# Value products for two quads at a time in a cross-attention kernel: a change read from its trace

## The chip, the cores and the metric

The kernel runs on one core of one Trainium2 chip. The metric is the device time of one execution in microseconds (us), taken as the median over runs. In the profile the engines are PE (TensorE matmul), PEld (TensorE weight load), DVE (VectorE), ACT (ScalarE), POOL (GpSimd) and SP (SyncE, which issues nearly all DMAs here).

## What is computed

The reference is a layer norm, a query projection, cross-attention with 32 heads over a context that serves as keys and as values, an output projection and a residual. Shapes: 8 batches, 256 query rows, 256 context rows, 1024 columns, everything in float32.

```python
x = (hidden - mean) * rsqrt(var + 1e-5) * gamma + beta
Q = split_heads(x @ Wq.T)                 # 32 heads of 32
K = V = split_heads(ctx)
scores = einsum('bhsd,bhtd->bhst', Q, K) * 32 ** -0.5
probs = softmax(where(mask, scores, -inf), axis=-1)
attn = einsum('bhst,bhtd->bhsd', probs, V)   # heads put side by side again
out = hidden + attn @ Wout.T
```

## The kernel before

**Quads and slots.** The work is cut into 64 quads: quad n is batch n // 8 and four heads (128 columns) of it. The main loop (L670) has 64 slots; the order of every instruction on every engine is the order in which the program writes it (L113), so what is queued where can be read from the loop body. Slot n does, on PE in this order: the scores of quad n+1 (`scores`, L354, tile `sc`), the value products of quad n-2 (`values`, L484, tile `pv`), a first group of output-product steps (`product_steps`, L543, tile `po`), one query projection for a quad some six slots ahead (`make_q`, L310, tile `pq`) and a second group of output-product steps. `STEPS` (L520) says how many steps fall in the two groups, by i = n % 8: for most batches (0,4), (0,3), (1,3), (1,2), (2,2), (2,1), (3,1), (0,3). The output product of a batch comes a batch later than its attention, as seven half-size products in Strassen's manner; its operand sums S1, S3, S2 (slot i = 1) and S4 (slot i = 2) are made by POOL (`sum_at`, L532). Float32 matmuls stand as two instructions each in the trace, so the 32 matmuls of `values` are 64.

**Softmax.** `softmax_parts` (L373) for quad n+1 runs in slot n, on four engines. For each of its four heads j, `exps(j)` has DVE take the masked scores out of PSUM with their row minimum (L396) and ACT exponentiate them with the row sums (L400). Then DVE makes the reciprocals (L407), POOL scales (L409), DVE transposes 32x32 blocks into `pT` (`blocks`, L415), and ACT puts half of `pT` aside in `pc` (`aside`, L421) so that two pairs of DMAs (L472, L476) can exchange partition groups. The loads due in the slot (`between`) are issued between the two pairs. DVE's order is exps(0), exps(1), exps(2), reciprocal 0, exps(3), reciprocal 1, blocks(0), and so on. ACT's order is exps(0), then the copies of finished value products out of PSUM (`copy_at`, L499, into `at`), then exps(1) to exps(3), aside, `copy_q`, aside. After the softmax, DVE makes the layer-norm statistics or blocks of a later batch, and POOL the sums.

**Buffers.** `sc` takes four PSUM banks, each for one head of a quad. `pv` has two banks (L104): a quad fills both, one for each half r of the partitions[...]. `pq` and `po` have a bank each. `pT` has three buffers, `pc` three. The mask of all batches is loaded by one DMA of 256 KB at the start (L186), as the seventh on the SP queue, ahead of the second x, of seven of the eight blocks of Wq and of the first values; `mask_bias` (L349) turns one batch of it into an additive bias.

**Evacuations.** A `po` bank is read by DVE (`keep` L561, `store` L569) or ACT (L559) before the next product may begin in it. In slots i = 2 and 3 DVE does this after exps(3) (`hooks[0]`), in slots i = 4, 5, 6 after blocks(0) (`hooks[1]`); the second group of steps of the slot waits for it. In the last batch's slots (56 to 63) the evacuation stands ahead of the softmax on DVE (L714). In slots above 58 there is no query projection left, and each slot adds one chunk of the last batch's own output projection (`project`, L572), for quads that are already copied to `at`. Values of the quads 62 and 63 and the rest of the projections follow the loop (L769 on).

The early slots (0 to 7) carry more: two query projections in some of them, POOL's folds of gamma into Wq (L342) and its sums of Wout blocks (L177).

Of the kernel before, what the change touches and what calls it, by code (L numbers as in the profile page):

```python
# [47 lines left out]
U8 = mybir.dt.uint8  # L48
# [11 lines left out]
def xattn_kernel(  # L60
# [34 lines left out]
    qp = ctx.enter_context(tc.tile_pool(name="qp", bufs=8))  # L95
    atp = ctx.enter_context(tc.tile_pool(name="atp", bufs=2))
    ep = ctx.enter_context(tc.tile_pool(name="ep", bufs=4))
    ptp = ctx.enter_context(tc.tile_pool(name="ptp", bufs=3))
    asp = ctx.enter_context(tc.tile_pool(name="asp", bufs=3))
    up = ctx.enter_context(tc.tile_pool(name="up", bufs=1))  # L100
    sm = ctx.enter_context(tc.tile_pool(name="sm", bufs=12))
    PS = bass.MemoryType.PSUM
    ps_s = ctx.enter_context(tc.tile_pool(name="ps_s", bufs=4, space=PS))
    ps_v = ctx.enter_context(tc.tile_pool(name="ps_v", bufs=2, space=PS))  # L104
# [33 lines left out]
    def load_v(n):  # L138
# [4 lines left out]
            vs[n], kv[b, g // 2, :, 2 * T :].rearrange("p (i v) -> p i v", i=NI)  # L143
        )

    def load_res(b, s, h):
        rs[b, s, h] = rp.tile([P, 512], F32, tag="r", name=f"r_{b}_{s}_{h}")
        nc.sync.dma_start(rs[b, s, h], x[b, ts(s, P), ts(h, 512)])
# [5 lines left out]
    mk = const.tile([P, B, T], U8, tag="mk", name="mk")  # L154
    NK = NC // 2
    wo = const.tile([P, 7, NK, 512], F32, tag="wo", name="wo")
    B11, B21, B22, T1, T2, T3, T4 = range(7)
# [191 lines left out]
    def mask_bias(b):  # L349

        mbs[b] = sm.tile([P, T], F32, tag="mb", name=f"mb_{b}", bufs=2)
        nc.vector.tensor_scalar(mbs[b], mk[:, b, :], 1.0, -MASKED, ALU.subtract, ALU.mult)

    def scores(n, part=range(NS)):  # L354
        if 0 in part:
# [17 lines left out]
    def softmax_parts(n, new_q=(), between=(), hooks={}, fill=()):  # L373
# [49 lines left out]
        if n == 0:  # L423
            for j in range(NH - 1):
                exps(j, (0,))
            yield
            exps(NH - 1, (0,))
            fill_in()
            yield
            for j in range(NH):  # L430
                exps(j, (1,))
            normalize(0)
            fill_in()
        else:
# [46 lines left out]
            tail()  # L481
        yield

    def values(n):  # L484
        pvs[n] = [
            ps_v.tile([P, 2, NS, K], F32, tag="pv", name=f"pv_{n}_{r}") for r in range(2)
        ]
        pT = pTs.pop(n)
        for i in range(NI):
            for j in range(NH):  # L490
                for r in range(2):
                    nc.tensor.matmul(  # L492
                        pvs[n][r][j * HD : (j + 1) * HD],
                        vs[n - n % 2][ts(r, 2 * K), i, ds(n % 2 * P + j * HD, HD)],
                        pT[ts(r, 2 * K), :, i, j, :, :],
                        start=(i == 0), stop=(i == NI - 1),
                    )

    def copy_at(n):  # L499
        b, c = divmod(n, NQ)  # L500
        if c == 0:
            ats[b] = atp.tile([P, NC, NS, NA, K], F32, tag="at", name=f"at_{b}")
        for r, pv in enumerate(pvs.pop(n)):
            nc.scalar.copy(  # L504
                ats[b][:, c, :, ts(r, 2), :], pv.rearrange("p a s k -> p s a k")
            )

# [88 lines left out]
        made += k  # L596


    loads, stats, norms, trans, moves, biases = ({n: [] for n in range(N)} for _ in range(6))
    for b in range(1, B):  # L600
        first = next(n for n in range(N) if b * NQ in new_qs[n])
        if b == 1:
            when = dict(moves=())
        elif b == 2:
            when = dict(
                loads=(0, 1), stats=(2, 3), norms=(3, 3), trans=(4, 4),
                moves=tuple(4 + i // 4 for i in range(16)),
            )
        else:
            when = dict(  # L610
                loads=(first - 12, first - 11), stats=(first - 10, first - 9),
                norms=(first - 8, first - 7), trans=(first - 7, first - 6),
                moves=tuple(first - 5 + i // 4 for i in range(16)),
            )
# [12 lines left out]


    sums = {n: [] for n in range(N)}
# [40 lines left out]
    for n in range(N):  # L670
# [156 lines left out]
```

## Time and profile before

| what | value |
|---|---|
| median of 3 runs | 595.76 us (595.75 to 595.84) |
| the profiled execution, its own time | 596.43 us |
| span of its profile | 594.6 us |
| PE busy | 582.0 us, 98% |
| PE weight loads busy | 389.3 us, 65% |
| DVE busy | 458.3 us, 77% |
| ACT busy | 407.0 us, 68% |
| POOL busy | 347.5 us, 58% |
| DMA queue of SP | 99.91 MB, 57.4% of 16 engines |

The span runs from the first instruction to the last; the execution's own time has 1.83 us more around it. A row of the profile gives an engine, a source line, the tiles written and read, a count, and the busy time. A row of the timeline gives the start, the length, and in brackets how long the engine sat idle before and what released it. Matmuls are pipelined, so neighbouring rows of PE overlap by some tenths of a microsecond; a group's cost is read from one start to the next. The granted clock is full in all slices of the profile.

### The profile page before, as it was taken

What the parts mean: (1) busy time and instruction counts of PE and PEld (TensorE: products, weight loads), DVE (VectorE), ACT (ScalarE), POOL (GpSimd) and SP (SyncE); (2) the same over time, 40 slices, a digit from 0 to 9 for tenths busy, and PEclk for the clock granted to TensorE, in tenths of its full rate; (3) what the DMA queues carried; (4) which work ended last, traced back from release to release, by engine and by line L of the source; (5) the groups of instructions that cost most, each with busy time, mean ns of one, the idle gap of its engine ahead of it and who ended that gap; (6) DMA issues with size and microseconds to landing.
All of it is one profiled execution on the core that took longest, in us unless ns stands there. A gap on an engine that the chain in (4) does not pass through costs nothing.

```text
span 594.6 us, 18914 instructions
## 1 busy us (share of the span) xinstructions
PE 582.0 (98%) x6680; PEld 389.3 (65%) x6680; DVE 458.3 (77%) x1675; ACT 407.0 (68%) x1380; POOL 347.5 (58%) x630
## 2 busy tenths in 40 slices
PE   9999999999999999999999999999999999999997
PEld 8787776666666676666676667666666667654443
DVE  5878888697887878788787887878787677779801
ACT  4788786776777776686676876677677677667700
POOL 1568896987557644755447653484556564385600
PEclk9999999999999999999999999999999999999999
DMA  8566798545863667544674457654556355466541
GB/s 309 222 165 210 227 255 234 156 114 172 228 185 90 175 177 209 167 113 139 195 225 128 130 157 191 193 155 136 158 145 194 99 162 142 125 181 174 165 126 71
DMA packets 42063, 101.13 MB, mean 170 GB/s; under 512 B 8560, under 2 KB 8560, under 8 KB 41968
## 3 DMA queue, kind: packets, MB, share of 16 engines
q1 hardware_dynamic: 41680, 99.91, 57.4%
q8 instruction: 53, 0.87, 0.7%
q14 instruction: 42, 0.34, 0.2%
q10 hardware_dynamic: 288, 0.01, 0.0%
HBM read 51.65 MB, written 8.39 MB: 101 GB/s over the span
## 4 chain that ended last, share of the span: by engine, by line
PE 76%; POOL 12%; DVE 5%; issue 2%; DMA 2%; ACT 2%; SPq 1%; POOLq 0%; DVEq 0%; ACTq 0%
PE pq L319 29%; PE po_S L549 17%; PE sc L362 9%; PE pv L492 9%; POOL e L409 8%; PE po_A L549 7%; PE po L577 3%; DVE e L396 2%; POOL wo L177 2%; POOL wq L342 1%; PE busy L118 1%; DMA pT<-pc 1%; DVE pT L415 1%; DVE st L211 1%; DMA v<-in_kv_dram 1%
## 5 line engine op out<-in xcount | busy, mean ns | idle before, releaser
L409 POOL TENSOR_SCALAR e<-e,rden 128x256 f32<-128x256 f32 x512 | 237.3, 481 | 172.3 <-DVE rden L407 168.7
L400 ACT ACTIVATE e<-e,mn 128x256 f32<-128x256 f32 x512 | 254.3, 502 | 55.2 <-DVE mn L396 55.2
L319 PE MATMUL pq<-xnT,wq 128*128 128x256 f32 (+1 forms) x1008 | 230.7, 382 | 1.3 <-ACT q L327 1.2
L415 DVE STREAM_TRANSPOSE pT<-e 128x512 f32<-128x512 f32 x256 | 181.4, 709 | 55.4 <-POOL e L409 48.2
L319 PEld LDWEIGHTS pq<-xnT,wq 128*128 128x128 f32 x1008 | 188.9, 190 | 45.1 <-issue 17.9
L396 DVE CUSTOM_DVE_ANT_0 e<-sc,mb 128x256 f32<-128x256 f32 x512 | 185.4, 417 | 33.8 <-PE sc L362 33.5
L421 ACT COPY pc<-pT 128x512 f32<-128x512 f32 x128 | 79.2, 619 | 76.1 <-DVE pT L415 45.3
L549 PE MATMUL po_S<-wo,at 128*128 128x512 f32 x224 | 107.0, 603 | 3.3 <-DVE u L561 1.3
L400 ACT ACTIVATION_READ_ACCUMULATOR e<-e,mn 128x1 f32 x512 | 98.4, 192 | 0.0
L492 PE MATMUL pv<-pT,v 64*32 64x128 f32 x4096 | 74.6, 274 | 2.2 <-DMA pT<-pc 1.4
L362 PEld LDWEIGHTS sc<-k,q 32*128 32x128 f32 x1024 | 46.4, 184 | 46.3 <-issue 23.4
L362 PE MATMUL sc<-k,q 32*128 32x256 f32 x1024 | 74.3, 401 | 0.1
L492 PEld LDWEIGHTS pv<-pT,v 64*32 64x32 f32 x4096 | 57.3, 105 | 25.0 <-issue 12.9
L549 PEld LDWEIGHTS po_S<-wo,at 128*128 128x128 f32 x224 | 40.6, 189 | 38.8 <-issue 31.8
L549 PE MATMUL po_A<-wo,at 128*128 128x512 f32 x112 | 52.0, 598 | 0.0
L407 DVE RECIPROCAL rden<-den 128x2 f32<-128x2 f32 x256 | 39.3, 153 | 9.0 <-ACT e L400 6.3
L396 DVE DVE_READ_ACCUMULATOR2_ANT mn<- 128x1 f32 x512 | 42.7, 83 | 0.0
L549 PEld LDWEIGHTS po_A<-wo,at 128*128 128x128 f32 x112 | 20.8, 190 | 19.1 <-issue 18.4
L217 POOL TENSOR_TENSOR rstd<-ve,mhalf 128x1 f32<-128x1 f32 x16 | 9.4, 585 | 38.8 <-DVE ve L216 38.2
L504 ACT COPY at<-pv 128x128 f32<-128x128 f32 x128 | 26.1, 253 | 8.1 <-PE pv L492 8.1
L333 ACT ACTIVATE q<-pq,qb 128x256 f32<-128x256 f32 x48 | 22.6, 470 | 10.2 <-PE pq L319 10.2
L549 PE MATMUL po_S<-wo,s 128*128 128x512 f32 x56 | 26.9, 605 | 0.6 <-DVE r L569 0.6
(52 smaller groups left out, 299.7 us busy)
## 6 DMA issues: line engine op xcount, KB each, us to landing
v<-in_kv_dram SPq DMA_DIRECT2D x32, 512.0 KB, 4.3
pT<-pT SPq DMA_DIRECT2D x128, 128.0 KB, 2.3
pT<-pc SPq DMA_DIRECT2D x128, 128.0 KB, 3.9
k<-in_kv_dram SPq DMA_DIRECT2D x32, 256.0 KB, 3.4
x<-in_x_dram SPq DMA_DIRECT2D x14, 512.0 KB, 5.6
r<-in_x_dram SPq DMA_DIRECT2D x28, 256.0 KB, 4.4
out_dram<-r SPq DMA_DIRECT2D x28, 256.0 KB, 3.1
xnT<-xe SPq DMA_DIRECT2D x96, 64.0 KB, 3.1
```

The source lines that it names most:

```text
L319: nc.tensor.matmul(pqs[n], wq[:, o, c, :], xnTs[b](c), start=(c == 0), stop=(c == NC - 1),)
L333: nc.scalar.activation(q[:, :S].rearrange("p (s a k) -> p a s k", s=NS, a=NA), pqs.pop(n).rearrange("p (a s k) -> p a s k", s=NS, a=NA), A ...
L362: nc.tensor.matmul(scs[n][j][:, s, :], qs[n][r, ts(s, P)], ks[n - n % 2][r, n % 2, :], start=True, stop=True,)
L396: nc.vector.tensor_tensor_reduce(out=e[:, s, :], in0=pss[j][:, s, :], in1=mbs[n // NQ], scale=1.0, scalar=NO_SCORE, op0=ALU.add, op1=ALU.m ...
L400: nc.scalar.activation(e[:, s, :], e[:, s, :], AF.Exp, bias=mn[:, s : s + 1], scale=-1.0, accum_out=den[:, s : s + 1],)
L407: nc.vector.reciprocal(rden, dens[j])
L409: nc.gpsimd.tensor_scalar(es[j][:, s, :], es[j][:, s, :], rden[:, s : s + 1], 1.0, ALU.mult, ALU.mult,)
L415: nc.vector.transpose(pT[:, :, :, j, :, :].rearrange("p a i s k -> p (a i) s k"), es[j].rearrange("p s (b t) -> p b s t", t=K),)
L421: nc.scalar.copy(pc[:, :, ts(j, 2)], pT[:, 1, :, ts(j, 2)])
L492: nc.tensor.matmul(pvs[n][r][j * HD : (j + 1) * HD], vs[n - n % 2][ts(r, 2 * K), i, ds(n % 2 * P + j * HD, HD)], pT[ts(r, 2 * K), :, i, j, ...
L504: nc.scalar.copy(ats[b][:, c, :, ts(r, 2), :], pv.rearrange("p a s k -> p s a k"))
L549: nc.tensor.matmul(pos[b], operand(b, name)[:, c], wo[:, which, c], start=begins and c == 0, stop=c == NK - 1, skip_group_check=not begins,)
```

## The change

`values` now takes quads as a group, and is called in the odd slots from 3 on, with the quads n-3 and n-2 together; the even slots have none. The two `pv` tiles hold both quads side by side[...]. `copy_at` copies both quads, four copies in one place of ACT's order instead of two. `pT` has four buffers for three, `pc` two for three, and the small softmax tiles eight for twelve. The mask comes as eight DMAs of 32 KB: the first where the whole mask stood, the others in the slots 8b - 5, within the loads between the two DMA pairs. In slot 63 the copies of quads 60 and 61 stand ahead of the chunk of the projection that reads quad 60. The calls after the loop, for the quads 62 and 63, stay single.

```diff
-    ptp = ctx.enter_context(tc.tile_pool(name="ptp", bufs=3))
-    asp = ctx.enter_context(tc.tile_pool(name="asp", bufs=3))
+    ptp = ctx.enter_context(tc.tile_pool(name="ptp", bufs=4))
+    asp = ctx.enter_context(tc.tile_pool(name="asp", bufs=2))
...
-    sm = ctx.enter_context(tc.tile_pool(name="sm", bufs=12))
+    sm = ctx.enter_context(tc.tile_pool(name="sm", bufs=8))
...
+    def load_mask(b):
+        mks[b] = sm.tile([P, T], U8, tag="mk", name=f"mk_{b}", bufs=2)
+        nc.sync.dma_start(mks[b], mask[:, b].to_broadcast([P, T]))
...
-    nc.sync.dma_start(mk, mask.to_broadcast([P, B, T]))
+    load_mask(0)
...
             for done in list(pvs):
-                copy_at(done)
+                copy_at(*done)
...
-    def values(n):
-        pvs[n] = [
-            ps_v.tile([P, 2, NS, K], F32, tag="pv", name=f"pv_{n}_{r}") for r in range(2)
+    def values(*quads):
+
+        pvs[quads] = [
+            ps_v.tile([P, len(quads), 2, NS, K], F32, tag="pv", name=f"pv_{quads[0]}_{r}")
+            for r in range(2)
         ]
...
+        for g, n in enumerate(quads):
+            pT = pTs.pop(n)
+            for i in range(NI):
+                for j in range(NH):
+                    for r in range(2):
+                        nc.tensor.matmul(
+                            pvs[quads][r][j * HD : (j + 1) * HD, g],
...
+    def copy_at(*quads):
+        pvr = pvs.pop(quads)
+        for g, n in enumerate(quads):
...
+            for r, pv in enumerate(pvr):
+                nc.scalar.copy(
+                    ats[b][:, c, :, ts(r, 2), :], pv[:, g].rearrange("p a s k -> p s a k")
+                )
...
+        masks[NQ * b - 5].append(b)
...
+        between += [partial(load_mask, one) for one in masks[n]]
...
-        if n >= 2:
-            values(n - 2)
+        if n >= 3 and n % 2:
+            values(n - 3, n - 2)
...
         else:
-            copy_at(n - 2)
+            copy_at(n - 3, n - 2)
```

More of the change, by code (lines that the diff above doesn't have):

```diff
@@ L144, in load_v @@
         )
+    mks = {}
+    def load_mask(b):
+        mks[b] = sm.tile([P, T], U8, tag="mk", name=f"mk_{b}", bufs=2)
+        nc.sync.dma_start(mks[b], mask[:, b].to_broadcast([P, T]))
     def load_res(b, s, h):
@@ L153, in xattn_kernel @@
     wq = const.tile([P, NC, NC, P], F32, tag="wq", name="wq")
-    mk = const.tile([P, B, T], U8, tag="mk", name="mk")
     NK = NC // 2
@@ L351, in mask_bias @@
         mbs[b] = sm.tile([P, T], F32, tag="mb", name=f"mb_{b}", bufs=2)
-        nc.vector.tensor_scalar(mbs[b], mk[:, b, :], 1.0, -MASKED, ALU.subtract, ALU.mult)
+        nc.vector.tensor_scalar(mbs[b], mks.pop(b), 1.0, -MASKED, ALU.subtract, ALU.mult)
     def scores(n, part=range(NS)):
@@ L482, in softmax_parts @@
         yield
-    def values(n):
-        pvs[n] = [
-            ps_v.tile([P, 2, NS, K], F32, tag="pv", name=f"pv_{n}_{r}") for r in range(2)
-        ]
[L488 to L506, printed above, removed]
+    def values(*quads):
+        pvs[quads] = [
+            ps_v.tile([P, len(quads), 2, NS, K], F32, tag="pv", name=f"pv_{quads[0]}_{r}")
+            for r in range(2)
+        ]
+        for g, n in enumerate(quads):
[5 more added lines that the diff above has]
+                            pvs[quads][r][j * HD : (j + 1) * HD, g],
+                            vs[n - n % 2][ts(r, 2 * K), i, ds(n % 2 * P + j * HD, HD)],
+                            pT[ts(r, 2 * K), :, i, j, :, :],
+                            start=(i == 0), stop=(i == NI - 1),
+                        )
+    def copy_at(*quads):
+        pvr = pvs.pop(quads)
+        for g, n in enumerate(quads):
+            b, c = divmod(n, NQ)
+            if c == 0:
+                ats[b] = atp.tile([P, NC, NS, NA, K], F32, tag="at", name=f"at_{b}")
+            for r, pv in enumerate(pvr):
+                nc.scalar.copy(
+                    ats[b][:, c, :, ts(r, 2), :], pv[:, g].rearrange("p a s k -> p s a k")
+                )
     PRODUCTS = (
@@ L596, in xattn_kernel @@
         made += k
-    loads, stats, norms, trans, moves, biases = ({n: [] for n in range(N)} for _ in range(6))
+    loads, stats, norms, trans, moves, biases, masks = (
+        {n: [] for n in range(N)} for _ in range(7)
+    )
     for b in range(1, B):
```

## The prediction, made before the change was run

> **What bounds the kernel now.** I read the page's busy shares first, then PE's timeline in a steady stretch, then what ends PE's few idle times, then the timelines of POOL, DVE and ACT around the places where PE would come earlier.
>
> ```profile
> PE 582.0 (98%) x6680; PEld 389.3 (65%) x6680; DVE 458.3 (77%) x1675; ACT 407.0 (68%) x1380; POOL 347.5 (58%) x630
> ...
> L492 PE MATMUL pv<-pT,v 64*32 64x128 f32 x4096 | 74.6, 274 | 2.2 <-DMA pT<-pc 1.4
> ```
>
> PE is busy nearly all the time, and the value products have 74.6 us of it, 1.17 us for each of 64 quads. What a burst costs is read from starts:
>
> ```profile
> 296.45 1.15 PE L362 MATMUL sc<-k,q 32*128 32x256 f32 x16
> 297.53 1.16 PE L492 MATMUL pv<-pT,v 64*32 64x128 f32 x64
> 298.61 3.72 PE L319 MATMUL pq<-xnT,wq 128*128 128x256 f32 x16
> 302.17 3.60 PE L549 MATMUL po_A<-wo,at 128*128 128x512 f32 x8
> 305.70 1.15 PE L362 MATMUL sc<-k,q 32*128 32x256 f32 x16
> 306.77 1.16 PE L492 MATMUL pv<-pT,v 64*32 64x128 f32 x64
> 307.86 3.72 PE L319 MATMUL pq<-xnT,wq 128*128 128x256 f32 x16
> ```
>
> Slots 32 and 33: scores to values 1.08, values to projection 1.08, no idle time. Slot 1 has no values, and its projection also starts 1.07 after its scores (29.36, 30.43): without a burst the slot is shorter by the burst's whole 1.08. In the steady stretch (132 to 527 us) PE is busy for 395.00 of 395.00 us. PE sets the pace there, in slots of 9.25 (even) and 8.39 (odd).
>
> It doesn't at both ends. From 58 to 128 us POOL's chain is nearly unbroken, and in slots 10 and 12 PE waits for it and for the DVE behind it; in slots 59 to 62 PE waits for an evacuation:
>
> ```profile
> 535.32 3.70 PE L549 MATMUL po_S<-wo,at 128*128 128x512 f32 x8 [0.64 <-DVE u L561]
> ...
> 565.02 1.31 PE L492 MATMUL pv<-pT,v 64*32 64x128 f32 x64 [0.85 <-ACT at L504]
> ```
>
> [...] 0.30 from the last score start to the first value start and 0.20 from the last value start to the next matmul, where value rounds of eight follow at 0.11. [...] DVE's first read of the scores begins 1.16 after the first score matmul, behind the last matmul into that bank, though half the bank was done earlier. So the copies of the first of two quads will wait for the second. [...]
>
> **The change, part by part** (us; minus is a gain).
>
> *Bursts merged.* A burst's 64 starts spread over 0.886 (eight rounds, the first 0.13, then 0.11). A removed burst saves 0.886 + 0.198 = 1.084 (the entry to the projection costs as much from the scores as the entry to values did). A quad appended to a running burst costs eight rounds of 0.109 = 0.872[...]. Bounds: 0.85 (0.106 a round) to 1.08 (no saving); I take 0.872. A pair of slots gains 0.212. All 31 would give 6.6.
>
> *The start, slots 2 to 12.* Here PE's time is not what ends.
>
> ```profile
> 64.58 1.28 POOL L177 TENSOR_TENSOR wo<-wo 128x512 f32<-128x512 f32 x1
> 65.80 0.18 POOL L341 COPY qb<-q 128x1 f32<-128x1 f32 x1
> 65.94 1.90 POOL L342 TENSOR_TENSOR wq<-wq,gam 128x1024 f32<-128x1024 f32 x1
> 67.82 3.67 POOL L409 TENSOR_SCALAR e<-e,rden 128x256 f32<-128x256 f32 x8
> ```
>
> These four repeat every 6.9 without a gap until 92. From there DVE and POOL hand each other normalize, statistics and sums until S2 ends at 108.21, where PE's `po_S` starts at 108.27, and until DVE's evacuation in slot 12 ends at 127.19, where the next group starts at 127.34. Nothing in that chain waits for PE. So PE's gain through slot 12 ends in longer waits there: 0. The wait of 1.4 for the DMA into `pT` in slot 4 goes, into the same sink. In slot 9 ACT's two extra copies (0.15 each) come before the exps POOL waits for: +0.3; slots 3 and 4 give +0.2 and -0.3. Together +0.2, from -0.8 (four pairs gained) to +1.2.
>
> *Slots 13 to 57.* 23 odd slots add 0.872 (20.06), 22 even ones drop 1.084 (23.85): -3.79.
>
> *ACT in odd slots.* The copies stand between exps(0) and exps(1). Before, they started 2.69 into a slot, when values were done. Now the last value matmul starts at 1.08 + 0.886 + 0.872 = 2.83, and a copy follows 0.31 later (as after the single bursts at the end), at 3.14: a wait of 0.45, then two more copies, 0.31. Behind them on ACT stand exps(1) to exps(3), +0.76; for them wait the reciprocals, POOL's scaling, blocks. In most slots this has room: an even slot has none of it, DVE ends at 8.03 of a slot that is now 9.26, and DVE's score reads end 4 to 5 before PE needs the banks. Two places have none, in the four batches with statistics (slots 16 to 47).
>
> Slot i = 2, S2:
>
> ```profile
> 315.42 0.55 POOL L217 TENSOR_TENSOR rstd<-ve,mhalf 128x1 f32<-128x1 f32 x1 [2.43 <-DVE ve L216]
> 315.93 1.28 POOL L539 TENSOR_TENSOR s<-at 128x512 f32<-128x512 f32 x1
> 317.29 1.28 POOL L539 TENSOR_TENSOR at<-at 128x512 f32<-128x512 f32 x1
> 318.65 1.27 POOL L539 TENSOR_TENSOR at<-s,at 128x512 f32<-128x512 f32 x1
> ...
> 320.68 2.74 PE L549 MATMUL po_S<-wo,at 128*128 128x512 f32 x6
> ```
>
> S2 ends 5.84 into slot 34; PE asks for it at 6.60. Now PE asks at 5.50. S2 is behind DVE's statistics, which are behind blocks(3) of slot 33, now 0.78 later, while slot 34 begins 0.87 later: it ends at 5.74, with 0.06 of handing over 0.30 late. Four batches: +1.2 (0 to 2).
>
> Slot i = 4, the evacuation:
>
> ```profile
> 337.48 0.65 DVE L561 TENSOR_TENSOR u<-po_S,p 128x512 f32<-128x512 f32 x1
> ...
> 339.17 1.88 PE L549 MATMUL po_S<-wo,at 128*128 128x512 f32 x4
> ```
>
> It ends 6.40 into slot 36; PE asks at 7.44, now at 6.36. Following DVE through slots 34 and 35 (blocks(3) then 0.08 later against the slot's start) gives 6.48, 0.18 late with the handing over: +0.7 (0 to 2).
>
> *Slots 58 to 62.* PE's gain is kept up to slot 58, whose scores start DVE's loop. Then a slot is 7.37: DVE's six score reads, a reciprocal, POOL's eight scalings, blocks(3), the evacuation. Removing a burst there gives nothing.
>
> ```profile
> 537.51 3.80 POOL L409 TENSOR_SCALAR e<-e,rden 128x256 f32<-128x256 f32 x8 [1.09 <-DVE rden L407]
> ```
>
> ACT's exps pairs (0.99) end just as POOL (0.95 a head) needs them: reciprocals start at 538.14, 539.13, 540.11, each as ACT ends. So 0.31 more of copies in slots 59 and 61 lengthens the loop by as much: +0.6; the even slots give none back, since POOL is full there.
>
> *The tail.* In slot 63 PE did values(61) and the chunk for quad 60 by 564.1, then waited for the copy of quad 61, that ACT, behind its last aside, began at 564.71. Now quad 60 is copied there too, and its chunk waits to 565.17; values(62) follow 1.05 later, at 566.2 for 565.02, less the 0.15 they then lost within the burst: +1.04 (0.8 to 1.3).
>
> *The mask.* 224 KB less in the first 12 us. PE's waits there are for ACT, DVE and POOL, and `mask_bias` began at 10.06 as DVE came free (10.02): 0 (-0.3 to 0.1). Seven later issues, about 0.35 each on SP (the first took 0.33), stand before `pT<-pc`, which is needed two slots later: 0; without that cover 7 x 0.35 = 2.5. The bias reads each mask a slot or more after its issue.
>
> *Buffers.* `pT` with four: blocks(0) of quad n+1 follow values(n-3), at the head of an odd slot, as before. `pc` with two: each is read out by its DMA two slots earlier; the nearest case is quad 4, whose aside began at 52.84 when quad 2's transfer had just landed (52.64). `sm`: nothing waits for it. 0 to +0.3.
>
> *Sum:* 0.2 - 3.79 + 1.2 + 0.7 + 0.6 + 1.04 = about 0. Of the profiled execution's 596.43 this leaves 596.4; the median lies 0.67 lower, so 595.7.
>
> **The rivals.** Within 0.2% is about what a measurement of this kernel can tell from no change (1.2 us).
>
> *A, as summed:* 595.7, by itself 594.6 to 596.9. 0.42.
>
> *B, the two waits at i = 2 and 4 don't arise* (DVE or ACT has slack that I booked as bound) and four pairs of the start are gained: 595.7 - 1.9 - 0.85 = 592.9. For it: only 0.2 to 0.3 each, from chains followed over three slots. Against: S2's chain has no idle time in it. 0.27.
>
> *B', PE's whole 6.6 arrives, less the tail's 1.04:* 596.43 - 0.67 - 5.56 = 590.2. Against: the waits at both ends. 0.08.
>
> *C, slower: ACT's four copies hold POOL's chain wherever it is the bound.* In slots 3, 5, 7 and 11 0.31 each (+1.2), and the evacuation at i = 4 is late by 0.48 for 0.18 (+1.2): 598.1. For it: the exps behind the copies feed every scaling. Against: POOL in slots 5 to 9 has queued work of its own. It decides from 0.79 of lateness per batch, with the rest as summed, since then the sum passes +1.2. 0.18.
>
> *D, the appended quad is not streamed* but costs a burst's 1.08 (the merge doesn't do what it says): 22 x 0.212 = 4.7 lost, 600.4. Nothing in the trace speaks for it. 0.05.
>
> **How the numbers follow.** Faster: B and B', 0.35. Same: A, 0.42. Slower: C and D, 0.23. The range reaches from a little below B to C, 592.6 to 598.2, and leaves out B', D and edges.
>
> **What would show it.** Right: even slots of 8.17 and odd ones of 9.26 where nothing waits; a double burst of 1.96; ACT's copies at 3.14 in slots i = 1, 5, 7; PE waiting about 0.3 for L539 and 0.2 for L561 in slots 16 to 47; slots 59 and 61 at about 7.7; the chunk of quad 60 waiting for ACT. Wrong: no PE wait in the steady stretch (B), slot 13 starting well before 129 (gains in the start), or slots 5 to 12 later by 1 or more (C).

## The result and the profile after

The changed kernel takes 600.0 us (597.61 to 601.29 in six executions) against 595.81 for the kernel before beside it: a ratio of 1.0063, interval 1.0043 to 1.0083. It is slower by 0.6%, outside the predicted range. A second series (e9 below) gave 599.82 against 595.67, ratio 1.0068 (1.0056 to 1.0080).

In eight of the eleven executions of the changed kernel (both series) the mean granted clock is 0.994 to 0.997. In the profiles such a mean goes with PE at half its clock for 3.41 us: 0.997 or 0.996 with one such stretch, 0.993 or 0.994 with two, or in e11 with one of 6.83. Of the 82 executions of the kernel before that stand beside the experiments one has a mean clock under 0.998 (0.997).

The page's busy shares and the group of the value products, after:

```profile
PE 580.1 (97%) x6680; PEld 389.7 (65%) x6680; DVE 456.5 (76%) x1675; ACT 408.0 (68%) x1380; POOL 347.7 (58%) x630
...
L500 PE MATMUL pv<-pT,v 64*32 64x128 f32 x4096 | 67.8, 273 | 0.5 <-DMA pT<-pc 0.5
```

The group's 74.6 us have become 67.8, yet the span grew from 594.6 to 599.5. The profiled execution itself took 601.29, the longest of the six, so the table below divides up the loss of that one execution. The span by stage, from the starts of the scores:

| stage | before | after | difference | predicted |
|---|---|---|---|---|
| start of slot 13 | 129.23 | 131.37 | +2.14 | +0.2 |
| slots 13 to 57 | 397.43 | 397.43 | 0.00 | -1.89 |
| slots 58 to 61 | 27.89 | 28.33 | +0.44 | +0.6 |
| slot 62 to the end | 40.08 | 42.38 | +2.30 | +1.04 |

**The steady stretch.** PE's timeline of slots 33 and 34 after the change (start, length, in brackets the idle time before):

```profile
307.58 1.15 PE L367 MATMUL sc<-k,q 32*128 32x256 f32 x16
308.66 2.10 PE L500 MATMUL pv<-pT,v 64*32 64x128 f32 x128
310.69 3.72 PE L324 MATMUL pq<-xnT,wq 128*128 128x256 f32 x16
...
316.92 1.15 PE L367 MATMUL sc<-k,q 32*128 32x256 f32 x16
...
318.96 3.62 PE L324 MATMUL pq<-xnT,wq 128*128 128x256 f32 x16
322.71 2.84 PE L559 MATMUL po_S<-wo,at 128*128 128x512 f32 x6
325.49 1.15 PE L367 MATMUL sc<-k,q 32*128 32x256 f32 x16
```

A double burst holds PE from 308.66 to 310.69, 2.03, where 1.96 was predicted. The odd slot is 9.34. The even slot 34 has no burst and would be 8.16, as the even slots with i = 0 and 6 are; it is 8.57, because the `po_S` group starts 3.75 after its projection instead of 3.45. No bracket stands there, since a matmul's modelled end covers the wait. What it waited for is in ACT's and POOL's timelines:

```profile
310.80 0.77 ACT L514 COPY at<-pv 128x128 f32<-128x128 f32 x4 [0.34 <-PE pv L500]
```

```profile
318.16 0.55 POOL L222 TENSOR_TENSOR rstd<-ve,mhalf 128x1 f32<-128x1 f32 x1 [2.43 <-DVE ve L221]
...
321.39 1.26 POOL L549 TENSOR_TENSOR at<-s,at 128x512 f32<-128x512 f32 x1
```

ACT's four copies start 3.22 into slot 33, and the next exponential follows them at 311.44 (before: the copies start 2.69 into the slot, and there are two). POOL's S2 then ends at 322.65, and PE's `po_S` follows at 322.71. This is the wait that the prediction placed here.

**The start.** ACT's, POOL's and PE's rows in slots 9 and 10 after the change, and SP's issue of the transfer out of quad 7's `pc`, first before and then after:

```profile
95.63 0.62 ACT L426 COPY pc<-pT 128x512 f32<-128x512 f32 x1 [5.02 <-DMA pT<-pc]
```

```profile
98.90 0.94 POOL L414 TENSOR_SCALAR e<-e,rden 128x256 f32<-128x256 f32 x2 [1.49 <-DVE rden L412]
100.54 2.89 POOL L414 TENSOR_SCALAR e<-e,rden 128x256 f32<-128x256 f32 x6 [0.70 <-DVE rden L412]
```

```profile
110.39 2.84 PE L559 MATMUL po_S<-wo,at 128*128 128x512 f32 x6 [1.78 <-POOL at L549]
```

```profile
84.49 1.92 SPq L476 DMA_DIRECT2D pT<-pc  x2
```

```profile
86.54 1.15 SPq L481 DMA_DIRECT2D pT<-pc  x2
```

ACT stands 5.02 for the DMA that reads `pc` out: quad 9 needs the buffer of quad 7, whose transfer SP issued at 86.54 (before: 84.49) and which had not landed. Behind the aside stand the exps of quad 10, which begin at 97.51 for 94.94, so POOL gets two holes of 1.49 and 0.70. Its scalings of the next slot begin at 110.32 for 108.19: these 2.13 are the start's whole loss in this execution.

**The end.** PE's two rows with the longest idle times after the change:

```profile
545.01 3.70 PE L559 MATMUL po_S<-wo,at 128*128 128x512 f32 x8 [1.91 <-DVE u L571]
...
560.01 5.37 PE L559 MATMUL po_S<-wo,at 128*128 128x512 f32 x8 [1.74 <-DVE r L579]
```

Where PE had waits of 0.64 to 0.73 before, one in each of the slots 59 to 62, it now has 1.91 and 1.74 in the slots 60 and 62, which have no burst. The second group takes 5.37 for the same eight matmuls that take 3.70 in the first: they step by 0.853 instead of 0.429. The granted clock is 0.5 from 560.53 to 563.94.

### The profile page after: what moved, and what is told of

The parts are those of the page before. It is cut to its first block, busy times and chain, and to the rows that moved or that the text cites. A ratio compares the mean times of both kernels' runs of the same rounds, so it can differ in the third digit from the quotient of the medians.

```text
span 599.5 us, 18868 instructions
## 1 busy us (share of the span) xinstructions
PE 580.1 (97%) x6680; PEld 389.7 (65%) x6680; DVE 456.5 (76%) x1675; ACT 408.0 (68%) x1380; POOL 347.7 (58%) x630
## 5 line engine op out<-in xcount | busy, mean ns | idle before, releaser
L559 PE MATMUL po_S<-wo,at 128*128 128x512 f32 x224 | 109.6, 615 | 7.2 <-DVE u L571 1.9
L500 PE MATMUL pv<-pT,v 64*32 64x128 f32 x4096 | 67.8, 273 | 0.5 <-DMA pT<-pc 0.5
L500 PEld LDWEIGHTS pv<-pT,v 64*32 64x32 f32 x4096 | 58.7, 105 | 13.0 <-issue 8.7
L514 ACT COPY at<-pv 128x128 f32<-128x128 f32 x128 | 24.4, 272 | 15.8 <-PE pv L500 15.8
```

The costliest lines, as they stand in the source:

```text
L500: nc.tensor.matmul(pvs[quads][r][j * HD : (j + 1) * HD, g], vs[n - n % 2][ts(r, 2 * K), i, ds(n % 2 * P + j * HD, HD)], pT[ts(r, 2 * K), : ...
L514: nc.scalar.copy(ats[b][:, c, :, ts(r, 2), :], pv[:, g].rearrange("p a s k -> p s a k"))
L559: nc.tensor.matmul(pos[b], operand(b, name)[:, c], wo[:, which, c], start=begins and c == 0, stop=c == NK - 1, skip_group_check=not begins,)
```

## The experiments

Four chips were used, one for each group of four. The kernel before had medians of 596.09, 595.72, 595.67 and 595.92 there, over 17 to 27 executions. The stages of each profiled execution, as in the table above, with the slots in which the clock was halved:

| kernel | median | ratio to before | slot 13 | 13 to 57 | 58 to 61 | 62 to end | half clock in slot |
|---|---|---|---|---|---|---|---|
| before | 595.81 | 1 | 129.23 | 397.43 | 27.89 | 40.08 | none |
| after | 600.0 | 1.0063 | 131.37 | 397.43 | 28.33 | 42.38 | 62 |
| e1 before, pc of two | 596.15 | 1.0000 | 129.22 | 397.30 | 27.85 | 40.04 | none |
| e2 after, pc of three | 597.99 | 1.0044 | 130.01 | 397.18 | 29.98 | 40.13 | 6, 60 |
| e3 after, end filled | 599.49 | 1.0068 | 130.62 | 397.40 | 28.32 | 41.07 | none |
| e4 after, single at the end | 598.21 | 1.0037 | 130.83 | 397.54 | 27.89 | 40.16 | 6 |
| e5 before, mask by batch | 596.90 | 1.0019 | 131.29 | 397.24 | 27.83 | 40.13 | 6 |
| e6 after, later quad first | 602.12 | 1.0102 | 130.44 | 400.12 | 29.91 | 40.13 | 6, 60 |
| e7 after, late copies | 594.79 | 0.9979 | 129.63 | 395.03 | 28.81 | 39.59 | 6 |
| e8 pairs mid, late, later first | 593.34 | 0.9958 | 128.94 | 395.86 | 27.45 | 39.88 | none |
| e9 after again | 599.82 | 1.0068 | 131.01 | 397.31 | 29.98 | 40.12 | 60 |
| e10 before, late copies | 594.62 | 0.9983 | 128.64 | 397.26 | 27.45 | 39.78 | none |
| e11 e7, slots 4 and 6 filled | 598.68 | 1.0048 | 134.80 | 394.91 | 28.82 | 39.58 | 7 |
| e12 pairs mid, late | 592.64 | 0.9958 | 128.48 | 394.69 | 27.45 | 39.88 | none |
| e13 after, mask 1 first | 598.95 | 1.0051 | 130.35 | 397.40 | 28.34 | 41.04 | 6 |
| e14 pairs alone | 599.27 | 1.0047 | 130.39 | 397.36 | 29.99 | 40.20 | 6, 60 |
| e15 after, late, pc of three | 593.99 | 0.9975 | 129.66 | 395.17 | 28.80 | 39.60 | 6 |
| e16 e12, mask 1 first | 592.45 | 0.9943 | 128.76 | 394.71 | 27.45 | 39.87 | none |

**The theories.** After the result: the pairs bring in the even slots what was forecast, and it is lost to four things: ACT's copies ahead of the exps, the second buffer of `pc`, waits within the burst, and the clock. The rival was one cause for all: that the pairs themselves, however served, cost the start and the end.

### First group: buffers, clock, end

**e1**, in the kernel before:

```diff
-    asp = ctx.enter_context(tc.tile_pool(name="asp", bufs=3))
+    asp = ctx.enter_context(tc.tile_pool(name="asp", bufs=2))
```

> The kernel before with two buffers of pc instead of three, nothing else. Theory (the third pc buffer is what the start loses: ACT's aside of quad 9 waits for the DMA that reads quad 7's pc): ACT waits about 5 us for pT<-pc near 95 us, slot 13 starts near 131 us instead of 129.2, and the time is 597.3 to 598.0 (1.5 to 2.2 over before). Rival (the four copies of value products on ACT delay POOL's chain in the start): the time stays at 595.8, within 0.3.

Measured: 596.15, ratio 1.0000 (0.9992 to 1.0008), and no ACT wait for that DMA. The expectation failed: two buffers are enough here, where quad 7's transfer is issued at 84.89.

**e2**, in the changed kernel; the three asides lie in a buffer of `at` that is not in use yet:

```diff
+        if n in (5, 7, 9):
...
+            pc = ats[1][:, ts(n % 4 // 2, NC // 2)].rearrange("p c s a k -> p (c s a k)")
...
+        else:
             pc = asp.tile([P, NI, NH, NS, K], F32, tag="pc", name=f"pc_{n}")
```

> The changed kernel with the pc tiles of quads 5, 7 and 9 in memory of the second at tile, which is not in use until slot 11, so that from quad 6 to 11 no pc is written again sooner than with three buffers. Theory (pc buffers): slot 13 starts at 129.2 to 129.6 us instead of 131.4 and the time is about 2 us below the changed kernel (597.5 to 598.3 where the granted clock drops as in it). Rival (four copies on ACT): slot 13 stays near 131, 600.0.

Measured: 597.99, ratio 1.0044 (1.0031 to 1.0057). ACT's wait is gone and slot 13 starts at 130.01, 1.36 earlier, though a half clock fell into slot 6. The median is where the theory had it. But the three executions at full clock took 597.8 to 598.0, where the changed kernel's two took 597.6 and 598.6. So part of the gain in the median may be fewer half clocks by chance.

**e3**, in the changed kernel: spare transposes, whose result nobody reads, in the slots where PE waits.

```diff
+        if n in (58, 60, 62):
+            spare = ps_v.tile([P, P], F32, tag="pv", name=f"spare_{n}")
+            for _ in range(16 if n > 58 else 6):
+                nc.tensor.transpose(spare, ident, ident)
```

> The changed kernel with idle PE time filled: 6 spare transposes in slot 58 and 16 in slots 60 and 62, between the scores and the output product, into a pv bank that is free there. Theory (the half clock from 560.5 to 563.9 us comes from PE's idle waits of 1.9 and 1.7 us in slots 60 and 62, which the merging makes out of four of 0.7): the clock stays full in every run, 597.5 to 598.6, and the runs agree within 0.5. Rival (the clock drop is chance and has nothing to do with the waits): some runs drop as before, median near 600.

Measured: 599.49, ratio 1.0068 (1.0054 to 1.0082). The profiled execution fits the clock theory: no half clock, and the last stage is 41.07 for 42.38, the +1.0 that the prediction had. The rest doesn't: three of five executions still have a mean clock of 0.997 (which slot it fell in isn't known for them), and the two at full clock (599.2 and 599.4) are no faster than the changed kernel's. The filling brought nothing in the median.

**e4**, in the changed kernel: single values from slot 56 on.

```diff
-        if n >= 3 and n % 2:
-            values(n - 3, n - 2)
+        if 3 <= n < 56:
+            if n % 2:
+                values(n - 3, n - 2)
+        elif n >= 56:
+            values(n - 2)
```

> The changed kernel with single value products in slots 56 to 63, as in the kernel before; the chunk of quad 60 no longer waits for its copy in slot 63. Theory: the end runs as before (slots 59 to 62 of 7.37, full clock, tail 40.0 from slot 62's start); of the 4.2 us lost 1.7 (clock), 1.0 (tail) and 0.4 (two extra copies in the loop) come back: 596.6 to 597.2. Rival (clock drop by chance): 1.4 comes back at most, 598.5.

Measured: 598.21, ratio 1.0037 (1.0024 to 1.0049). The end is the kernel before's again (27.89, 40.16), but the median misses the theory's 597.2 and is nearer to the rival's 598.5. The remaining loss of the profiled execution is the start's 1.60, with a half clock in it. The execution at the full mean clock of 1.0 is the slowest here (598.72), so the clock is not all that sets the executions apart.

### Second group: mask, order, place of the copies

**e5**, the kernel before with the change's `load_mask` and nothing else of it.

> The kernel before with only the mask loaded batch by batch; its first odd slots issue one DMA more than the kernel before (slot 3). The theory after the first four runs is that the start's loss comes from two buffers of pc together with the doubled value products; then this kernel stands at 595.5 to 596.2 with slot 13 at 129.2 and no ACT wait for the DMA out of pc. The rival: the extra DMA in slot 3 shifts the whole queue of SP, which issues in order, and with it the transfers of slots 7 to 12; then 597 to 598 and slot 13 at 130.2 or later.

Measured: 596.90, ratio 1.0019 (1.0009 to 1.0029). Its executions fall in two: seven with a mean clock of 0.999 or 1.0 at 595.5 to 597.2, five with 0.996 or 0.997 at 597.7 to 598.3. In the profiled one the clock is halved in slot 6 (its mean is 0.86 from 66 to 72 us and 0.89 from 72 to 80): slot 5 began a microsecond earlier (60.12 for 61.10), PE came earlier to ACT's copy in slot 6 and waited 1.11 for it. Slot 13 is 2.06 late there, with no pairs and with three buffers of `pc`. At full clock the median is 596.17, 0.45 over the kernel before. The median of all lies between theory and rival, and the rival's shift of the transfers is there (that out of quad 7's `pc` is issued at 85.95 for 84.49). So the mask's DMAs cost little by themselves, but they move transfers, and PE to where it stands idle.

**e6**, in the changed kernel:

```diff
-        for g, n in enumerate(quads):
+        for g, n in reversed(list(enumerate(quads))):
```

> The changed kernel with the later quad of a pair multiplied first, so that a wait for its transfers, if one is needed, stands ahead of the burst and not within it. Theory: the semaphore waits in PE's queue ahead of the second quad cost 0.075 per double burst, so bursts of 1.835 (first start to last) become 1.760 as in slots i = 3, odd slots become 9.26, and 22 of them give 1.6 us: median about 598.2, slot 57 less slot 13 at 385.6 instead of 387.2. Rival: the lost 0.075 belongs to the switch to another tile of probabilities and values[...], wherever the waits stand; then bursts stay at 1.83 and the time within 0.5 of the changed kernel.

Measured: 602.12, ratio 1.0102 (1.0079 to 1.0125). The burst's starts now span 1.76 or 1.77 in 23 of 31 and most odd slots are 9.26, so the 0.075 did come from waits ahead of the second quad, and the theory's reason held. But four bursts of the stretch 13 to 57 stop, and their starts span 2.58 to 2.91, 0.8 to 1.15 more. One of them, in e6:

```profile
343.27 1.98 PE L500 MATMUL pv<-pT,v 64*32 64x128 f32 x122
345.96 0.42 PE L500 MATMUL pv<-pT,v 64*32 64x128 f32 x6 [0.71 <-issue]
```

"issue" says that no semaphore in the profile held it; what else the profiles show at such stops is in the last section. Both theories missed the time.

**e7**, in the changed kernel:

```diff
             exps(0)
             while tails:
                 tails.pop()()
-            for done in list(pvs):
-                copy_at(*done)
             exps(1)
             exps(2)
             normalize(0)
             exps(3)
+            for done in list(pvs):
+                copy_at(*done)
```

> The changed kernel with the copies of the value products placed behind the four exps on ACT instead of behind the first. Theory: what the late copies hold is exps(1) to exps(3); without that the wait of 0.30 ahead of S2 in slots 18, 26, 34, 42 is gone (1.2) and the loop of slots 58 to 62 is back at 27.9 (0.4): slot 57 less slot 13 at 386.0, median about 598.3 to 598.9. Rival: the wait at i = 2 comes from the shorter even slot alone, not from ACT; then it stays at 0.3, and the copies, now later, hold PE's next products in the odd slots, so that the time is the changed kernel's or worse.

Measured: 594.79, ratio 0.9979 (0.9970 to 0.9988): 5 us faster than the changed kernel by one move, and faster than the kernel before (though not than that kernel with the same move, e10). PE in slot 34 of e7, and POOL's S2 ahead of it:

```profile
316.09 3.62 PE L324 MATMUL pq<-xnT,wq 128*128 128x256 f32 x16
319.54 2.74 PE L559 MATMUL po_S<-wo,at 128*128 128x512 f32 x6
```

```profile
317.59 1.27 POOL L549 TENSOR_TENSOR at<-s,at 128x512 f32<-128x512 f32 x1
```

S2 ends at 318.86, 0.68 before PE asks. All even slots of the stretch are 8.16, those with i = 2 and with i = 4: the copies' place caused both waits, in this kernel with its shorter slots. The rival (that the shorter slot alone causes them) is out. I had expected 1.2 from this and it gave 2.40, because the evacuations at i = 4 go with it and each wait lengthened its slot by more than PE's bare stall. The start gave 1.74, and the end was 2.3 better, 1.3 of it for the lack of a half clock there.

**e8**, pairs in slots 14 to 55 only, with the edits of e2, e6 and e7.

> All mended together: pairs in slots 14 to 55 only, single values at the start and at the end, three buffers of pc for the quads 5, 7 and 9, the later quad first, copies behind the exps. If the losses add up as booked (start 0 to 0.3 worse than before, the stretch 13 to 57 at 388.2 less 21 pairs of 0.212 = 383.8 to 384.2, end as before), the time is 591.6 to 592.6. Rival: the freed time of PE turns into new waits in the middle (evacuations and S2), so that half of it or less arrives: 593.8 to 595.5.

Measured: 593.34, ratio 0.9958 (0.9945 to 0.9971), between theory and rival. Start and end are better than before; the middle falls short because two bursts stop as in e6 (2.85 and 2.95 in place of 1.76).

### Third group: whose gain is it, and the clock again

**e9**, the changed kernel once more.

> The changed kernel once more, beside the three that follow. Theory: its executions fall apart by the clock alone: without a stretch of half clock 597.6 to 598.8, with one about 1.7 to 2 more, with two 600 or more; median 598.5 to 600.2. Rival: the spread has another cause, and executions at a full mean clock (0.999 or 1.0) reach over 599.5.

Measured: 599.82. By mean clock: 598.9 (1.0), 599.8 and 600.2 (0.997), 599.4 and 599.8 (0.994). The execution at full clock is the fastest, as expected, but two half clocks cost no more than one here. A possible reason, not tested by a run: ACT's longest wait for the DMA out of `pc` is 3.9 to 5.0 in the three profiles without a half clock in slot 6 (after, e9, e3) and 0 to 3.4 in those with one (e6, e13, e7, e4). So the two losses of the start may partly take each other's place.

**e10**, in the kernel before, the same move of the copies as in e7.

> The kernel before with only the order of ACT changed: the copies of the value products behind the four exps. Theory: in the kernel before the two copies have room where PE is the bound, so the late place brings nothing in the steady stretch (slots 13 to 57 at 388.2, as before) and at most 0.3 in the start: 595.2 to 596.1. Then what the late place gave the changed kernel (5.2) was the cost of the change's own four copies. Rival: the late place is a gain by itself, whatever the values do, as in the start, where POOL's chain waits for the exps: 594.5 or less.

Measured: 594.62, ratio 0.9983 (0.9977 to 0.9990), all 21 executions within 594.5 to 595.3. The expectation failed, and the rival's cause held, though its 594.5 was just missed: the place of the copies costs the kernel before 1.05 as well, by the profiles 0.6 in the start, 0.44 in the loop of slots 58 to 61 and 0.3 behind it, but 0.17 in the steady stretch. So about one of e7's five microseconds undoes nothing of the change, and e7 (0.9979) is not clearly faster than this kernel (0.9983): pairs in all slots show no gain in the median even with late copies.

**e11**, e7 with 13 spare transposes in slots 4 and 6, where PE waits 1.5 for ACT.

> The changed kernel with late copies and, in slots 4 and 6, 13 spare transposes on PE between the scores and the projection, where it waits 1.5 for ACT (work whose result nobody reads). Theory: the half clock of slot 6 follows on PE's waits there, so no execution has a mean clock under 0.998 and the profile has no projection step of 0.427 in slot 6; the slow half of the times with late copies only (594.8 to 595.7) goes: median 593.3 to 594.3. Rival: the half clock doesn't depend on this wait, or its time is hidden behind POOL's chain: the same mean clocks and a median of 594.8 again.

Measured: 598.68, ratio 1.0048 (1.0034 to 1.0062), a plain miss. The wait in slot 6 is filled and its half clock is gone, but PE then stops in slot 7 for 3.65 with the reason "issue" (81.48 to 85.13), and the clock is halved from within that stop (its mean is 0.82 from 82 to 85, 0.50 from 85 to 90, 0.93 from 90 to 95). The experiment tells nothing on the cost of slot 6.

**e12**, e8 without its edit of e6: the earlier quad first.

> Pairs in slots 14 to 55 only, single values in the start and at the end, three buffers of pc for quads 5, 7, 9, copies late, the earlier quad first. Theory: the wait of 1.0 within some bursts that came with the later quad first is gone, bursts are at 1.84, slots 13 to 57 at 388.2 less 21 times (0.212 - 0.075) = 385.3; start and end as in the kernel before: 592.0 to 593.0. Rival: the order of the quads doesn't matter for the sum, since the waits come back elsewhere: 593.3, as with the later quad first.

Measured: 592.64, ratio 0.9958 (0.9944 to 0.9972). The bursts' stops are gone and the middle is 394.69, with 21 pairs at (397.26 - 394.69) / 21 = 0.122 each against e10. Five executions lie at 592.1 to 593.9, one at 595.1 with a clock of 0.997. Against e10, on the same chip and with the copies in the same place, the pairs, with the rest of the change, are worth 2.0 us in the median; all 21 at the forecast 0.212 would be 4.5.

### Fourth group: which part costs the start

**e13**, in the changed kernel: the mask of batch 1 at the start.

```diff
     load_mask(0)
+    load_mask(1)
...
-        masks[NQ * b - 5].append(b)
+        if b > 1:
+            masks[NQ * b - 5].append(b)
```

> The changed kernel with the mask of batch 1 loaded at the start, beside that of batch 0, so that slot 3 has no DMA more than before (those of batches 2 to 7 as in the change). Theory: the DMA in slot 3 is what makes slot 5 begin early, PE wait in slot 6 at half clock, and SP issue the transfer out of pc of quad 7 two us later (86.5 for 84.5), for which ACT waits 4 to 5 in slot 9; without it slot 13 starts at 129.2 to 130.0 and the median is 597.4 to 598.4. Rival: the pairs shift the transfers, not the mask: ACT's wait for the DMA out of pc stays at 3 us or more, slot 13 at 131, and the median at 599.5 to 600.

Measured: 598.95, ratio 1.0051 (1.0039 to 1.0063), half-way between the two. ACT's wait for `pc` is 1.0, but the profiled execution has the half clock in slot 6, with which the mask in slot 3 gave 0 to 3.4 as well, so that alone tells nothing. Three of five executions have a half clock as before, and those at full clock (597.5, 598.7) are no better than the changed kernel's. So the mask's DMA in slot 3 is not what the half clocks need, and what it costs in time isn't shown by this run; what it does to the transfer is told below.

**e14**, the edits of e2 and e13 together, so that of the change's part in the start only the pairs and their copies are left.

> The changed kernel with both by-works of the change undone as far as the start goes: mask of batch 1 at the start, and a third buffer of pc for quads 5, 7, 9. What is left is the pairs with their four copies in one place. Theory: the start is at most 0.5 worse than before (copies), slots 13 to 57 give 1.0, slots 57 to the end cost 2.3 to 2.8 without a half clock: 596.6 to 597.9 where no half clock falls in; with one at the end 1.3 more. Rival: the pairs alone already cost the start its 2: 598.5 or more.

Measured: 599.27, ratio 1.0047 (1.0033 to 1.0061). At full clock 597.5 twice, with one half clock 598.8, with two 599.7 to 599.8 three times: the executions at full clock are where the theory had them, the median where the rival had it. PE around slot 6, and the table by stretches (busy time of each engine, then PEclk, DMA share and GB/s), in e14:

```profile
65.97 2.11 PE L368 MATMUL sc<-k,q 32*128 32x256 f32 x16
69.62 8.83 PE L325 MATMUL pq<-xnT,wq 128*128 128x256 f32 x32 [1.54 <-ACT q L335]
78.39 0.93 PE L368 MATMUL sc<-k,q 32*128 32x256 f32 x12
```

```profile
69.00:74.00 5.00, 4.38 (x13) 3.58 (x14) 4.85 (x21) 3.76 (x14) 5.00 (x8) 0.66 0.73 251
```

In slot 6 a single burst used to stand in the time in which ACT finishes its copy; now PE waits 1.54 and the clock falls to 0.66 of full in the mean of the 5 us. The 32 matmuls take 8.83 where they took 7.15 before. So the half clock came in slot 6 with the pairs and without a mask in slot 3, behind a wait of 1.54; in e5 it came with this mask and without pairs, behind one of 1.11.

**e15**, the changed kernel with the edits of e2 and e7.

> The changed kernel with late copies and three buffers of pc for the quads 5, 7 and 9. Theory: with the copies out of the exps' way and no wait for pc, the start ends as early as in the kernel before with late copies (128.6) if no half clock falls into slot 6, and up to 1 later with it: 592.5 to 594.0. Rival: what is late in the start by then is the half clock and SP's queue, not pc: 594.3 to 595.3, as with late copies only (594.8).

Measured: 593.99, ratio 0.9975 (0.9966 to 0.9983): seven executions at 0.999 or 1.0, six of them at 593.2 to 594.0 and one at 595.25, four at 0.996 with 595.0 to 595.4. The median is at the upper edge of the theory's range. One half clock costs some 1.3 here.

**e16**, e12 with the mask of batch 1 at the start.

> Pairs in slots 14 to 55, late copies, three buffers of pc for quads 5, 7, 9, and the mask of batch 1 at the start. Theory: the one execution of eight at 595.1 with a lower clock that the same kernel had with the mask in slot 3 came from slot 6; without it all executions are at 592.0 to 593.0. Rival: it came from elsewhere: one in four or so at 594 or more again.

Measured: 592.45 (592.21 to 592.77), ratio 0.9943 (0.9931 to 0.9955). No execution has a lower clock. That is what the theory said, but with one such execution of six in e12 (the expectation's eight is a slip), none of five may be chance, and the intervals of e12 and e16 overlap. It is the lowest ratio of all and beats both kernels, by 3.5 us and, taking the ratios, by some 7. Of the 3.5 about 1 is the late copies' (e10) and not the pairs'. Slots 32 and 33 of e16 show the pairs at work without a wait:

```profile
295.08 1.15 PE L368 MATMUL sc<-k,q 32*128 32x256 f32 x16
...
303.24 1.15 PE L368 MATMUL sc<-k,q 32*128 32x256 f32 x16
304.32 2.11 PE L507 MATMUL pv<-pT,v 64*32 64x128 f32 x128
306.36 3.72 PE L325 MATMUL pq<-xnT,wq 128*128 128x256 f32 x16
```

## Why the prediction was wrong

The sum of the prediction was about 0, and the profiled execution came out 4.9 longer. Three of its terms were too small: the appended quad (+20.06, measured +21.66), the two waits behind ACT's copies (+1.9, measured +2.45) and the buffers (0 to 0.3, measured 2.1 in the start). A fourth, the clock, had no term at all (1.3 in slot 62).

**The worth of a removed burst was right.** Even slots without a wait came out at 8.16, predicted 8.17. The forms of loss that were named also came: waits at i = 2 and i = 4, the loop, the tail.

**The appended quad was sized 0.07 too low.** In the odd slots the predicted 9.26 comes only where i = 3, five times of 23; elsewhere a slot takes 9.34 or a little more. The second quad brings waits on the DMA semaphores into the burst, two instructions of 0.051 each in PE's queue, and four rounds take 0.115 to 0.133 for 0.109. e6, with the other order, puts them ahead of the burst and has 9.26. Over the odd slots the sum is +21.66 for +20.06, a miss of 1.60. The pair's gain is so 0.12 to 0.14, not 0.212.

**ACT's copies: right in kind, too small.** The slots lengthened by 0.40 at i = 2 and 0.21 at i = 4, together 2.45 in four batches, for 1.2 + 0.7. With the even slots at -24.1 without them, the sum is -21.65 for -21.95. Stretch 13 to 57 so lost all: 21.66 - 21.65 = 0.0. PE's own lateness at i = 2 was 0.30, as predicted (3.75 for 3.45); the slot lost 0.10 more. e7 shows that the waits go with the copies' place.

**The buffers were wrong.** "The nearest case is quad 4", at most 0.3. I followed when a buffer is read out in the timeline of before; but the transfer of quad 7 was issued two microseconds later in the changed kernel, and ACT was let go nine microseconds after its issue, in a stretch where the DMA engines are nearly full (DMA share 0.91 from 86 to 92, 1.01 from 92 to 98; in the kernel before 0.99 and 0.91). ACT's 5.02 made POOL's 2.13. e1 shows that the buffer alone costs nothing, e2 that with a third one the wait is gone. What shifts the transfer can be read from the profiles: it is issued at 85.5 to 87.2 in all 12 with the mask's DMA in slot 3 (86.54 in the changed kernel, 85.95 in e5, which has no pairs) and at 83.3 to 85.4 in all six without it. Three pairs of kernels differ by the place of that DMA alone: e13 and after (85.40, 86.54), e14 and e2 (84.54, 86.88), e16 and e12 (83.33, 85.53); e5 differs from the kernel before (84.49) by the loading of the mask alone. So two parts of the change that were booked as 0 act together: the mask's DMA delays the transfer by 1.1 to 2.3, and with two buffers ACT has to wait for it. Why one DMA more delays it by that much stays open. The share of the loss is open too: less 1.3 for its half clock the profiled execution is 600.0, 1.4 to 2.4 over the two of its series at full clock, so a loss of 2.1 in the start isn't there in each.

**The start was booked as a sink.** "Nothing in that chain waits for PE" holds for the chain, but PE's longer waits were not free: behind the one of 1.54 in slot 6 of e14 the clock was halved for 3.41. No step of the prediction had the clock in it. Its price: 1.3 for one stretch in the executions of e14 and e15, 2.2 for two in e14; in the profiles 1.3 in slot 62 (42.38 for 41.07, e3) and 1.65 in slot 60 (29.98 in e9 for 28.33). In e4 the order of the executions doesn't follow it. The changed kernel's executions at full clock took 597.6, 598.6 and 598.9, the others 599.4 to 601.3. So without any half clock the change would still have lost 1.8 to 3.2 us.

**Mask: 0 was nearly right for the time it takes** (0.45 at full clock in e5), wrong for what it moves: the transfer out of `pc`, and PE's place in slot 6 (e5: half clock in 5 of 12 executions, +2).

**Loop and tail: right.** +0.44 for +0.6; +1.0 for +1.04 in e3, and 1.3 more where the half clock falls in slot 62.

**Rival C** was the nearest: the copies do hold POOL's chain, and its 598.1 is about what the changed kernel takes at full clock. But of its two places, the start's four slots were not where the time went in the profile (the slot 9 buffer was), and i = 4 was late by 0.21, not 0.48. Rival D's 600.4 hit the number by luck, for a reason that is not there (and with 23 odd slots in place of its 22 it would be 600.6).

The same idle time does not always go with a half clock: e16 waits 1.7 in slot 4 without one. What the profiles say on this stands in the last section.

## What to carry to other kernels

Before merging work on the pacing engine, follow what stands behind its consumer: the copies doubled in one place of ACT's queue took back 2.45 of the 3.79 that the steady stretch was to gain, and moving them behind the four exps gave 5 us in all, one of which the kernel before gains by it too. A saving on an engine that then waits elsewhere can be worse than nothing: behind the longer, rarer waits (1.1 to 1.9 in the profiles) PE's clock was halved in many executions (a mean of 0.994 to 0.997 in eight of eleven), so keep single bursts where PE isn't the bound, as e16 does. A buffer's slack read from the old timeline holds only as long as no transfer is issued later, so every part of a change that adds a transfer ahead of it counts.

## What the runs showed of the hardware

**The clock was halved behind waits of 1.1 to 1.9.** The stretches at half clock are 3.413 us long (after: 560.53 to 563.94; one in e11 is twice that). PE, with work on both sides, idled 1.11 ahead of the one in e5, 1.54 in e14 and 1.89 in e9, and four of the six executions of e14 have a mean clock of 0.994 or 0.997. In the profile of the kernel before no stretch of 3.41 us between 20 and 588 us has more than 1.35 of idle time, and the granted clock is 1.0 from 6.72 to 593.81. That the waits bring the half clock is inferred from this and not shown: e3 and e11 filled waits, and three of five and five of six of their executions still have means of 0.994 to 0.997.

**The half clocks lie on a grid of 3.413 us.** In each profile with several stretches at half clock (the one at the very end counted) they start whole multiples of 3.413 apart: after at 560.53 and 598.08 (11 times), e14 at 69.91 and 544.37 (139 times). So in these profiles the clock changes on a grid of such steps. The wait of 1.9 in slot 60, in e9 and e13:

```profile
544.52 5.40 PE L559 MATMUL po_S<-wo,at 128*128 128x512 f32 x8 [1.89 <-DVE u L571]
```

```profile
543.98 3.70 PE L560 MATMUL po_S<-wo,at 128*128 128x512 f32 x8 [1.92 <-DVE u L572]
```

In e9 the wait lies within one step (541.79 to 545.20), and the clock is halved from 545.20; in e2, e6 and e14 it is the same. In e13 a line of the grid at 543.78 cuts it, in the changed kernel one at 543.46, which leaves 1.71 and 1.55 in the step: both stay at full clock there. Idle time alone doesn't rank the steps, though: behind 1.11 in slot 6 of e5 the clock was halved. What else counts was not shown.

**PE stopped where no semaphore held it.** The profile after lists a DMA queue of the kind "instruction" apart:

```profile
q8 instruction: 53, 0.87, 0.6%
```

Its packets are of 16 KB (53 for 0.87 MB). In ten stops of PE marked "issue", in five kernels, the count of PE's earlier instructions in the trace (loads, matmuls and semaphore waits) is 1729 (after, e9, e3: slot 8; e11: slot 7), 4545, 7873, 9921 and 11201 (e6), 6593 and 11201 (e8): always apart by whole multiples of 256. In each, PE goes on 2.2 to 2.9 us after a packet of this queue started (after: the packet at 82.57, PE at 85.27, behind a stop of 0.44). A double burst is 128 weight loads and 128 matmuls, 256 in all, over in 2.0 us: in e6 at 343.27 the packet started with the burst (343.25) and PE stood from 345.25, six matmuls before the burst's end, to 345.96. That PE waited for these packets is inferred from counts and times and not shown; no run changed the program's length to move the stops on purpose, though with e11's 26 added transposes the stop at 1729 falls in slot 7 instead of slot 8.
